# Slack for named consumers in an engine plan, a second buffer for the second products, and places of sorted tokens counted in two levels

## The chip, the core and the metric

The kernel runs on one core of one Trainium2 chip. The engines of the core run side by side, each with an instruction queue of its own that is worked off in order: TensorE (PE in the profile; PEld is its weight loading), VectorE (DVE), ScalarE (ACT), GpSimd (POOL) and SyncE (SP), which here only issues DMAs. The metric is the device time of one execution in microseconds. The time before is 2369.66 us, the median of three runs (2361.89 to 2370.21).

## The reference, cut to what matters

```python
# x: 32 images, 128 channels, 56 x 56 pixels, float32
x = x + conv3x3(sign(group_norm(x)), sign(w)) * Alpha        # w from M, Z, rv
t = x as tokens                                              # 32 x 3136 x 128
n = layer_norm(t)
t = t + (n @ Wq + bq) * sum_over_tokens((n @ Wk + bk) * (n @ Wv + bv))
n = layer_norm(t)
p = softmax(n @ router_w + router_b)                         # 8 experts
top_p, top_i = top_k(p, 2);  top_p = top_p / sum(top_p)
t = t + sum_k top_p[k] * (n @ expert_w[top_i[k]] + expert_b[top_i[k]])
x = t as images
```

## The kernel before, in words

**Units.** An image has 3136 tokens, cut into 25 chunks of 128 (the last has 64) and 7 blocks of four chunks (the last has one). The images form four groups of 8, 8, 8 and 4 (`GROUPS`), and four more that belong to no group.

**The first part of an image.** Its two halves are loaded (L296), the sum and the sign of the group norm are taken on ScalarE (`gn_sum` L511, `gn_sign` L531), the convolution is 7 x 9 matmuls (L565), which VectorE adds to x (L576). PE turns x into tokens (`to_tokens` L592), ScalarE copies them out (L598), VectorE takes statistics (L605). ScalarE scales the tokens (L656), PE sums their products (`gram` L665), some small steps (`kv_1` to `kv_8`) make the vector that the queries are multiplied with, and `project` (L780) with its two followers (L794, L806) ends the attention.

**The experts, two ways.** The router is computed on VectorE. The first 8 chunks of an image in groups 0 and 1, the first 12 in groups 2 and 3 (`DENSE`) and all 25 of the last four images take the dense way: for each block and each pair of experts, SP issues a DMA that spreads two rows of gates over the partitions (`spread`, tile `bc`, L1044), VectorE multiplies the turned tokens with them (`gated`, L1053, two buffers), and PE multiplies by the two expert matrices (`experts`, L1071, into the bank `ff`).

The other chunks (17 or 13 per image) take the sorted way. `pair_of` on VectorE numbers the pair of experts of each token (28 pairs) and writes a 0/1 array `hot` (chunk x pair, L1163). `places` on PE counts, by matmuls into one bank, how many tokens of the same pair come ahead of a token: one matmul with a triangle for the chunk's own tokens (L1174), two for the images before (L1177), and for each chunk c one with ones that adds its counts to all later chunks (L1186). ScalarE copies the new counts (`count_on`), VectorE forms row numbers (`row_numbers`), and GpSimd scatters the tokens to their rows in DRAM (L1253).

When a group is sorted, its rows are read back as tiles of 128 rows of one pair, four tiles (a quad) at a time, 40, 40, 32 and 20 quads in the groups. The steps of a quad are:

- `tile_load`, SP: four DMAs (L1517) into `t_in`, three buffers
- `tile_turn`, PE: four transposes (L1524); `tile_turned`, ScalarE: the copy out (L1530, tile `turned`, two buffers)
- `tile_experts`, PE, in two halves: products with the two expert matrices of the pair (L1542, tile `to`)
- `tile_read`, ScalarE, in two halves: the first products scaled and shifted into `v` (L1560), the second scaled into `w` (L1567, one buffer)
- `tile_sum` and `tile_out`, VectorE: v + w (L1572) and the tokens added (L1577)
- `tile_store`, SP: the store to `res` (L1585)

Then GpSimd gathers the results of each image (`gather`, L1323, rows found by `result_rows`), PE turns them (`back_turn`, L1338), ScalarE copies them out (`back_out`, L1346, tile `o`) and SP stores them (L1350).

**The order.** The order of every engine's queue is made on the host, ahead of the build. Each step is announced with `at(...)`: a due time, its engine, a guess of its work, the steps that it comes `after`, the rings of buffers that it takes (`take`) and frees (`free`), and a `delay` after which a DMA counts as landed. `in_order` plays this plan through: on each engine it takes, of the steps that could start about now, the one with the earliest due time. A step can start when what it waits for is done, plus a hop of 0.5 to 0.8. `ROOM` says how many buffers of each ring the plan counts on. The plan decides nothing but the order: on the chip each instruction starts when its engine has come to it and its semaphores are there. The line that the change edits in `in_order` is

```python
f.ready = max(f.ready, clock[s.engine] if same else s.done + HOP[f.engine])
```

where s is the step just placed and f one that waits for it; `same` is true when both are on one engine.

## Time and profile before

The profiled execution took 2367.37 us, with a span of 2365.7 us from its first to its last instruction; 1.7 us lie around the span.

| engine | busy us | share of the span | instructions |
|---|---|---|---|
| PE | 2146.5 | 91% | 12074 |
| DVE | 1959.7 | 83% | 6332 |
| ACT | 1519.5 | 64% | 4883 |
| POOL | 1029.2 | 44% | 971 |

The mean granted TensorE clock is 0.971 of full speed. Matmuls are pipelined and their ends are modelled, so a busy PE need not be PE at its peak. The groups that the change is about:

| group | count | busy us | mean ns |
|---|---|---|---|
| PE L1186, matmuls of `places` | 428 | 51.8 | 276 |
| PE L1542, products of the quads | 2112 | 291.8 | 286 |
| ACT L1530, turned quads copied | 132 | 81.1 | 616 |
| ACT L1560, first products | 528 | 252.9 | 479 |
| ACT L1567, second products | 528 | 206.0 | 390 |
| DVE L1572, v + w | 132 | 90.8 | 688 |
| DVE L1053, gated, 128 x 1024 | 368 | 445.6 | 1214 |
| DVE L1163, `hot`, 128 x 476 | 16 | 10.3 | 646 |

A float32 matmul is recorded as two instructions, so 2112 records are 1056 products. An engine that waits does so in its own order: whatever is queued behind the waiting instruction waits with it.

### The profile page before, as it was taken

What the parts mean: (1) busy time and instruction counts of PE and PEld (TensorE: products, weight loads), DVE (VectorE), ACT (ScalarE), POOL (GpSimd) and SP (SyncE); (2) the same over time, 40 slices, a digit from 0 to 9 for tenths busy, and PEclk for the clock granted to TensorE, in tenths of its full rate; (3) what the DMA queues carried; (4) which work ended last, traced back from release to release, by engine and by line L of the source; (5) the groups of instructions that cost most, each with busy time, mean ns of one, the idle gap of its engine ahead of it and who ended that gap; (6) DMA issues with size and microseconds to landing.
All of it is one profiled execution on the core that took longest, in us unless ns stands there. A gap on an engine that the chain in (4) does not pass through costs nothing.

```text
span 2365.7 us, 44856 instructions
## 1 busy us (share of the span) xinstructions
PE 2146.5 (91%) x12074; PEld 1476.3 (62%) x12074; DVE 1959.7 (83%) x6332; ACT 1519.5 (64%) x4883; POOL 1029.2 (44%) x971
## 2 busy tenths in 40 slices
PE   4999999998999989998999999999998989989878
PEld 2766656566677666666676676666667656665533
DVE  4899999998988877997788878999877787778755
ACT  5767765567877777667777766666777846563311
POOL 1054443432333313755544454666644553343562
PEclk9999999999999999999999999999999999999989
DMA  4155434465564544576667766677676766867678
GB/s 163 43 176 176 151 131 136 153 192 152 178 187 151 156 134 143 170 228 205 202 206 218 214 174 195 221 221 255 202 236 172 240 193 203 261 207 231 212 225 272
DMA packets 317739, 448.55 MB, mean 190 GB/s; under 512 B 61065, under 2 KB 223153, under 8 KB 317490
## 3 DMA queue, kind: packets, MB, share of 16 engines
q1 hardware_dynamic: 289090, 386.97, 52.3%
q0 software_dynamic: 27392, 55.17, 7.8%
q10 hardware_dynamic: 1008, 3.54, 0.4%
q8 instruction: 101, 1.65, 0.3%
q14 instruction: 148, 1.21, 0.2%
HBM read 319.51 MB, written 126.00 MB: 188 GB/s over the span
## 4 chain that ended last, share of the span: by engine, by line
PE 35%; DVE 19%; DMA 11%; ACT 9%; issue 5%; SPq 2%; POOL 1%; DVEq 0%; ACTq 0%; POOLq 0%
PE ff L1071 12%; PE cv L565 6%; PE to L1542 4%; DVE gated L1053 4%; PE gram L665 3%; PE q L780 3%; DMA back<-res,res_no 3%; DMA x<-in_x_dram 2%; DMA bc<-gp 2%; ACT v L1560 2%; DVE tok L732 2%; ACT w L1567 2%; ACT y L656 1%; DVE st L605 1%; DMA rows<-tok,row_no 1%
## 5 line engine op out<-in xcount | busy, mean ns | idle before, releaser
L1253 POOL DMA_INDIRECT rows<-tok,row_no x428 | 523.7, 1223 | 780.3 <-issue 221.8
L1071 PE MATMUL ff<-gated,ew_d 128*128 128x512 f32 (+1 forms) x1536 | 719.8, 597 | 34.2 <-DVE gated L1053 34.1
L1323 POOL DMA_INDIRECT back<-res,res_no x428 | 496.2, 1159 | 519.7 <-PE back_ps L1338 335.0
L1053 DVE TENSOR_TENSOR gated<-tt,bc 128x1024 f32<-128x1024 f32 x384 | 450.1, 1175 | 66.7 <-PE ff L1071 52.3
L565 PE MATMUL cv<-xs,w_bin 128*128 128x448 bf16 x2016 | 433.6, 359 | 10.0 <-ACT w L1567 4.6
L1071 PEld LDWEIGHTS ff<-gated,ew_d 128*128 128x128 f32 x1536 | 274.7, 194 | 263.0 <-issue 189.6
L1542 PE MATMUL to<-ew_s,turned 128*128 x2112 | 291.8, 286 | 50.4 <-ACT turned L1530 46.3
L1542 PEld LDWEIGHTS to<-ew_s,turned 128*128 128x128 f32 x2112 | 269.8, 198 | 91.7 <-ACT turned L1530 59.6
L1560 ACT ACTIVATE v<-to,t_in 128x128 f32<-128x128 f32 x528 | 252.9, 479 | 109.0 <-PE to L1542 106.2
L794 ACT ACTIVATE qs<-q,r 128x136 f32<-128x136 f32 (+1 forms) x800 | 247.7, 406 | 98.7 <-PE q L780 91.0
L565 PEld LDWEIGHTS <-w_bin 128*128 128x128 bf16 x2016 | 197.4, 99 | 175.5 <-issue 28.1
L656 ACT ACTIVATE y<-tok,r 128x128 f32<-128x128 f32 (+1 forms) x800 | 250.9, 411 | 52.9 <-DVE r L476 42.0
L665 PEld LDWEIGHTS gram<-y 128*128 128x128 f32 (+1 forms) x1600 | 212.0, 197 | 61.3 <-ACT y L656 31.1
L780 PE MATMUL q<-move,x 128*128 128x144 f32 (+1 forms) x1600 | 237.2, 292 | 8.4 <-ACT w L1567 7.1
L665 PE MATMUL gram<-y 128*128 128x129 f32 (+1 forms) x1600 | 226.5, 286 | 14.7 <-ACT y L656 14.7
L780 PEld LDWEIGHTS q<-move,x 128*128 128x128 f32 (+1 forms) x1600 | 212.6, 191 | 34.7 <-issue 14.6
L1567 ACT ACTIVATE w<-to,t_in 128x128 f32<-128x128 f32 x528 | 206.0, 390 | 3.7 <-DVE v L1572 3.7
L605 DVE BATCH_NORM_STATS2 st<-tok 128x6 f32<-128x128 f32 (+1 forms) x800 | 180.5, 276 | 23.6 <-ACT tok L598 22.8
L1572 DVE TENSOR_TENSOR v<-v,w 128x512 f32<-128x512 f32 x132 | 90.8, 688 | 122.0 <-ACT w L1567 121.5
L813 DVE BATCH_NORM_STATS2 st<-tok 128x6 f32<-128x128 f32 (+1 forms) x800 | 189.1, 276 | 0.0
L598 ACT COPY tok<-xt 128x512 f32<-128x512 f32 (+1 forms) x224 | 118.1, 566 | 75.2 <-PE xt L592 71.6
L576 DVE SCALAR_TENSOR_TENSOR x<-cv,alpha_col,x 128x448 f32<-128x448 f32 x224 | 150.9, 674 | 16.6 <-PE cv L565 14.7
(214 smaller groups left out, 2935.0 us busy)
## 6 DMA issues: line engine op xcount, KB each, us to landing
bc<-gp SPq DMA_DIRECT2D x368, 512.0 KB
x<-in_x_dram SPq DMA_DIRECT2D x64, 784.0 KB
t_in<-rows SPq DMA_DIRECT2D x528, 66.0 KB
res<-v SPq DMA_DIRECT2D x132, 256.0 KB
out_dram<-o SPq DMA_DIRECT2D x100, 256.0 KB
out_dram<-tt SPq DMA_DIRECT2D x92, 256.0 KB
rows<-zeros SPq DMA_DIRECT2D x116, 66.0 KB
rows<-tok,row_no POOLq DMA_INDIRECT x428
```

The lines of the kernel that those rows point to most:

```text
L565: nc.tensor.matmul(cv, lhsT=w_bin[:, t, :], rhs=xs[:, b * ROWS + dy : b * ROWS + dy + ROWS, dx : dx + width], start=(t == 0), stop=(t == T ...
L656: nc.scalar.mul(y[:n, j, :C], d["tok"][:n, c, :C], d["r1"][:n, c : c + 1])
L665: nc.tensor.matmul(d["gram"], lhsT=y[:n, j, :C], rhs=y[:n, j, :], start=(c == 0), stop=(c == n_ck - 1),)
L780: nc.tensor.matmul(p[:n, k, :], lhsT=d["x"][:, c * C : c * C + n], rhs=move, start=True, stop=True,)
L794: nc.scalar.mul(qs[:n, k, : C + N_EXP], p[:n, k, : C + N_EXP], d["r1"][:n, c : c + 1])
L1053: nc.vector.tensor_tensor(g[:, :, :n], d["tt", b][:, :n].unsqueeze(1).to_broadcast([C, 2, n]), d.pop(("bc", b, k))[:, :, :n], ALU.mult,)
L1071: nc.tensor.matmul(d["ff", b][:, :n], lhsT=ew_d[:, e * C : (e + 1) * C], rhs=g[:, j, :n], start=False, stop=(e == N_EXP - 1),)
L1253: dma = nc.gpsimd.indirect_dma_start(out=groups[group]["rows"], out_offset=bass.IndirectOffsetOnAxis(ap=d["row_no"][:n, c - n_dense : c - ...
L1323: dma = nc.gpsimd.indirect_dma_start(out=d["back", c][:n, :], out_offset=None, in_=groups[group]["res"][: quads_of(group) * WIDE, :], in_o ...
L1542: nc.tensor.matmul(p[:, k, j, :], lhsT=t[:, n * C : (n + 1) * C], rhs=ew_s[:, bass.ds(d["cols", q][j][n], C)], start=True, stop=True,)
L1560: nc.scalar.activation(d["v", q][:, n, :], p[:, k, 0, :], AF.Identity, bias=row[:, C + 2 : C + 3], scale=row[:, C : C + 1],)
L1567: nc.scalar.mul(d["w", q][:, n, :], p[:, k, 1, :], row[:, C + 1 : C + 2])
```

## The change

A step gets one more number, `slack`. In the plan a step on another engine can start only `slack` later than it could before; the chip does not see it, only the order moves. It is 2.0 for `tile_read`, 1.0 for `tile_turned` and 0.5 for `gated`. The time at which a ring's buffer comes free in the plan is not moved by it. `tile_turn` of a quad is now placed after the second half of `tile_experts` two quads back. The `delay` of the loads of x goes from 9 to 13.

The tile `w` gets two buffers, in the plan and on the chip. The tile `o` goes from three buffers on the chip to the two that the plan counted on.

`pair_of` gets one more VectorE instruction, a reduction of `hot` over each four chunks (`hot_sum`, bfloat16). `places` adds the counts of a chunk only to the later chunks of its own four, and the sum of four to all chunks behind them. The guesses of work for both now go with the number of chunks.

```diff
@@ -84,16 +84,17 @@
 BANKS, EMPTIES = ("ps", "acc", "ff"), 7.0
 ROOM = dict(
     x=3, tok=3, ps=5, acc=1, ff=2, y=3, qs=3, tt=4, bc=4, gt=2, gated=2,
-    t_in=3, turned=2, v=3, w=1, back=12, sent=4, o=2,
+    t_in=3, turned=2, v=3, w=2, back=12, sent=4, o=2,
 )
 
 
 class Step:
 
 
-    def __init__(self, due, key, engine, work, do, args, after, take, free, delay):
+
+    def __init__(self, due, key, engine, work, do, args, after, take, free, delay, slack):
         self.due, self.key, self.engine, self.work = due, key, engine, work
-        self.do, self.args, self.delay = do, args, delay
+        self.do, self.args, self.delay, self.slack = do, args, delay, slack
         self.after, self.take, self.free = after, take, free
         self.done = None
 
@@ -156,7 +157,7 @@
             missing[f.key] -= 1
 
             same = f.engine == s.engine and (not s.delay or f.key[0] == s.key[0])
-            f.ready = max(f.ready, clock[s.engine] if same else s.done + HOP[f.engine])
+            f.ready = max(f.ready, clock[s.engine] if same else s.done + s.slack + HOP[f.engine])
             if not missing[f.key]:
                 waiting.setdefault(f.engine, []).append(f)
     return order
@@ -403,6 +404,7 @@
 
 
     hot_all = const.tile([C, most + 1, N_PAIR], BF16, name="hot")
+    hot_sum = const.tile([C, most // PER, N_PAIR], BF16, name="hot_sum")
 
     def prepare_sorted():
         nc.gpsimd.memset(hot_all, 0.0)
@@ -437,8 +439,8 @@
 
     steps = {}
 
-    def at(due, key, engine, work, do, *args, after=(), take=(), free=(), delay=0.0):
-        steps[key] = Step(due, key, engine, work, do, args, after, take, free, delay)
+    def at(due, key, engine, work, do, *args, after=(), take=(), free=(), delay=0.0, slack=0.0):
+        steps[key] = Step(due, key, engine, work, do, args, after, take, free, delay, slack)
 
     def base(i):
 
@@ -538,7 +540,7 @@
         at(
             s - 60, ("load", i), "SP", 0.1, load,
             after=[("load", i - 1)] + ([("gn_sign", 0, GN_PARTS - 1)] if i == 1 else []),
-            take=["x"], delay=9.0 if i else 19.0,
+            take=["x"], delay=13.0 if i else 19.0,
         )
         for j in range(GN_PARTS):
             rows = j * height // GN_PARTS, (j + 1) * height // GN_PARTS
@@ -1116,7 +1118,7 @@
                     begin + n * unit, ("gated", i, n), "DVE", 1.14 * share, gated, b, k,
                     after=[("spread", i, n), ("tt_out", i, b)]
                     + [("gated", i, n - 1) if n else ("gated", i - 1, last_unit)],
-                    take=["gated"], free=[("bc", ("spread", i, n))],
+                    take=["gated"], free=[("bc", ("spread", i, n))], slack=0.5,
                 )
                 at(
                     begin + n * unit + 2, ("experts", i, n), "PE",
@@ -1143,6 +1145,7 @@
         first_of_group = i == 0 or group_of[i - 1] != group
         sort = slice(n_dense, n_ck)
         hot = hot_all[:, most - n_sort :, :]
+        n_full = n_sort // PER
 
         def pair_of():
             high, low, pair = (
@@ -1166,6 +1169,13 @@
                 pair_no.unsqueeze(1).to_broadcast(shape),
                 ALU.is_equal,
             )
+            with nc.allow_low_precision(reason="numbers up to four"):
+                nc.vector.tensor_reduce(
+                    hot_sum[:, :n_full, :],
+                    hot[:, : n_full * PER, :].rearrange("p (b k) q -> p b q k", k=PER),
+                    AX.X,
+                    ALU.add,
+                )
 
         def places():
 
@@ -1181,14 +1191,17 @@
                         start=False,
                         stop=False,
                     )
-            for c in range(n_sort):
-                n = n_sort - c
+
+            counted = [(hot[:, c, :], c + 1, min(n_sort + 1, c // PER * PER + PER)) for c in range(n_sort)]
+            counted += [(hot_sum[:, b, :], (b + 1) * PER, n_sort + 1) for b in range(n_full)]
+            counted = [(t, lo, hi) for t, lo, hi in counted if lo < hi]
+            for t, lo, hi in counted:
                 nc.tensor.matmul(
-                    p[:, c + 1 :, :],
+                    p[:, lo:hi, :],
                     lhsT=ones_h,
-                    rhs=hot[:, c, :].unsqueeze(1).to_broadcast([C, n, N_PAIR]),
+                    rhs=t.unsqueeze(1).to_broadcast([C, hi - lo, N_PAIR]),
                     start=False,
-                    stop=c == n_sort - 1,
+                    stop=lo == counted[-1][1] and hi == counted[-1][2],
                 )
             d["places"] = p
 
@@ -1261,11 +1274,11 @@
             alone(f"rows{group}", dma, in_turn(dma))
 
         at(
-            s + 132, ("pair_of", i), "DVE", 0.87, pair_of,
+            s + 132, ("pair_of", i), "DVE", 0.9 + 0.03 * n_sort, pair_of,
             after=[("route_3", i), ("row_numbers", i - 1), ("places", i - 1), ("result_rows", i - 13)],
         )
         at(
-            s + 133, ("places", i), "PE", 2.1, places,
+            s + 133, ("places", i), "PE", 0.3 + 0.08 * n_sort, places,
             after=[("pair_of", i), ("count_rest", i - 1), ("list_1", group - 1)], take=["ps"],
         )
         at(s + 135, ("count_rest", i), "DVE", 0.11, count_rest, after=[("count_on", i)])
@@ -1342,7 +1355,7 @@
 
         def back_out(b):
             lo, hi = cols_of(b)
-            d["o", b] = bpool.tile([C, WIDE], F32, tag="o", name=f"o_{i}_{b}")
+            d["o", b] = bpool.tile([C, WIDE], F32, tag="o", bufs=2, name=f"o_{i}_{b}")
             nc.scalar.copy(d["o", b][:, : hi - lo], d.pop(("back_ps", b))[:, : hi - lo])
 
         def back_store(b):
@@ -1552,7 +1565,7 @@
         d = groups[g]
         if h == 0:
             d["v", q] = bpool.tile([C, PER, C], F32, tag="v", name=f"v_{g}_{q}")
-            d["w", q] = bpool.tile([C, PER, C], F32, tag="w", bufs=1, name=f"w_{g}_{q}")
+            d["w", q] = bpool.tile([C, PER, C], F32, tag="w", bufs=2, name=f"w_{g}_{q}")
         p = d.pop(("to", q, h))
         for k in range(2):
             n = 2 * h + k
@@ -1624,11 +1637,12 @@
             )
             at(
                 due, ("tile_turn", g, q), "PE", 0.45, tile_turn, g, q,
-                after=[("tile_load", g, q), ("tile_turn", g, q - 1)], take=["ps"],
+                after=[("tile_load", g, q), ("tile_turn", g, q - 1), ("tile_experts", g, q - 2, 1)],
+                take=["ps"],
             )
             at(
                 due + 1, ("tile_turned", g, q), "ACT", 0.47, tile_turned, g, q,
-                after=[("tile_turn", g, q)], take=["turned"], free=[("ps", ("tile_turn", g, q))],
+                after=[("tile_turn", g, q)], take=["turned"], free=[("ps", ("tile_turn", g, q))], slack=1.0,
             )
             for h in range(2):
                 at(
@@ -1639,7 +1653,7 @@
                 at(
                     due + 3 + 2 * h, ("tile_read", g, q, h), "ACT", 1.40, tile_read, g, q, h,
                     after=[("tile_experts", g, q, h), ("tile_read", g, q, h - 1)],
-                    take=[] if h else ["v", "w"], free=[("ps", ("tile_experts", g, q, h))],
+                    take=[] if h else ["v", "w"], free=[("ps", ("tile_experts", g, q, h))], slack=2.0,
                 )
             at(
                 due + 9, ("tile_sum", g, q), "DVE", 0.60, tile_sum, g, q,
```

## The prediction

> **What bounds the kernel now.** I read the page's busy times and slices first, then the waits by engine, then the stretches in which tiles are read back, then the chain.
>
> ```profile
> PE 2146.5 (91%) x12074; PEld 1476.3 (62%) x12074; DVE 1959.7 (83%) x6332; ACT 1519.5 (64%) x4883; POOL 1029.2 (44%) x971
> PE   4999999998999989998999999999998989989878
> PEclk9999999999999999999999999999999999999989
> PE 35%; DVE 19%; DMA 11%; ACT 9%; issue 5%; SPq 2%; POOL 1%; DVEq 0%; ACTq 0%; POOLq 0%
> ```
>
> PE is busy nearly everywhere, and the chain of work has PE as its largest owner, but with many short stays on other engines: PE is the bound, with stalls. It was idle for 2365.7 - 2146.5 = 219 us; 29 of them lie at the start. The waits say whom it waited for (engine, line, releaser: us in total, times, longest):
>
> ```profile
> PE to L1542 <- ACT turned L1530: 46.3, 23, 5.5
> PE ff L1071 <- DVE gated L1053: 34.1, 27, 4.1
> PE places L1174 <- DVE hot L1163: 14.0, 11, 2.8
> PE q L780 <- ACT w L1567: 7.1, 4, 2.8
> PE cv L565 <- ACT w L1567: 4.6, 4, 2.5
> DVE v L1572 <- ACT w L1567: 121.5, 59, 5.9
> ACT w L1567 <- DVE v L1572: 3.7, 4, 2.1
> ACT o L1346 <- DMA out_dram<-o: 44.6, 10, 11.4
> ACT junk L511 <- DMA x<-in_x_dram: 39.9, 19, 6.0
> SPq L1517 <- DVE v L1577: 202.3, 66, 10.0
> ```
>
> The largest stall of PE is a quad's product waiting for its turned tile. VectorE stands 121.5 us in front of the sum of a quad. SP stands 202.3 us in front of quad loads, until `t_in` is free. By stretches (length; busy of PE, PEld, DVE, ACT, POOL; clock, DMA share, GB/s):
>
> ```profile
> 540.00:900.00 360.00, 328.06 (x2024) 245.61 (x2023) 300.78 (x971) 274.08 (x886) 109.18 (x88) 0.95 0.54 163
> 1080.00:1440.00 360.00, 331.53 (x2040) 244.99 (x2041) 289.38 (x889) 265.47 (x840) 168.34 (x148) 0.98 0.68 202
> 60.00:540.00 480.00, 449.39 (x2530) 300.68 (x2529) 450.62 (x1688) 325.02 (x1096) 189.65 (x149) 0.98 0.46 147
> 1440.00:1680.00 240.00, 233.75 (x1269) 153.34 (x1268) 232.21 (x800) 151.53 (x498) 147.76 (x120) 0.99 0.68 222
> ```
>
> The first two are stretches with tile reading: PE loses 9 and 8%, and no other engine is over 84%. The last two have none: PE and VectorE are both at 94 to 97%, and nothing much can be won there.
>
> **Turned tiles: 27 us won (10 to 42).** What hides the copy of a turned quad is the PE work queued between `tile_turn` and the first `tile_experts`. From the order of both kernels and the trace's durations (convolution 1.83, gated pair 1.74, `gram` block 0.89, half a quad 0.90, `project` 0.74, transposes 0.44) this cover has a mean of 3.2 us before and 3.9 after; it is below 2.0 in 27 of 132 quads before and in none after, below 2.5 in 45 and 6. The copy takes 0.62 itself, so what made 23 quads wait 2.0 each is copies queued behind other ACT work. If waits go with the quads below 2.5, 23 x 6/45 = 3 stay, 6 us: 40 won, and with the 1.9 us that the same line shows under issue at most 42. If ACT's queue is what is late, a median cover grown by 0.9 (2.9 to 3.8) takes 23 x 0.9 = 21 off; 10 is half of that. I take 27.
>
> **Places: 10 us won (-16 to +25), and 3 at its start (0 to 9).** With 17 chunks, L1186 adds 17 x 18/2 = 153 chunk columns of 28; after, 25 in thirteen narrow matmuls and 32 in four wide ones. With 13 chunks it is 91 against 37. The instructions stay at 17 and 13. Seventeen took 2.0 us in the trace for 4284 columns. Whether narrow ones are cheap:
>
> ```profile
> L1186 PE MATMUL places<-hot,ones_h x10: 175/229/282, 872.4 to 873.1; 128*128 128x280 bf16 x1, 128*128 128x252 bf16 x1, 128*128 128x224 bf16 x1, 128*128 128x196 bf16 x1
> ```
>
> The last ten, 280 columns down to 28, start within 0.7 us, and nine of them stream 1512 columns, 0.46 ns each: no floor shows down to some 30 ns. So an image with 17 comes to 1596 x 0.46 = 0.73, and 0.1 for the floor: 1.1 us less, or 0.6 less with 13. 16 x 1.1 + 12 x 0.6 = 25 us of PE, the upper bound. [...]
>
> VectorE pays for the reduction. The trace has no such form; the nearest row is the reduction of 476 float32 elements to 17 (L1207), 647 ns, hence 0.61 for 448 elements and 0.46 for 336: 16 x 0.61 + 12 x 0.46 = 15 us, 16 as the loss if VectorE is the bound throughout and PE's gain is worth nothing. It is not: only 11 of 28 images (0 to 6 and some four later) fall in stretches where VectorE is as full as PE. There I count the two as even. The other 17 keep 25 x 17/28 = 15, less about a third for places where another wait ends last: 10. PE need not wait for the reduction: the triangle, the two counts and thirteen narrow matmuls, over 1 us, read `hot` alone. The plan's guess for `pair_of` rises from 0.87 to 1.41, so `places` is put later behind it, against the 14.0 us (11 times) that PE waits for `hot`; 3 of these.
>
> **Slack of 2.0 behind readings, and two `w`: 8 us won (0 to 30).** Between the end of a reading and its sum the plan now puts 3.6 VectorE steps on average (2.0 before), so most of the 121.5 us goes. It is idle time of an engine that is not the bound there (84%). PE pays for it only where it waits for VectorE in these stretches: `gated` 7.4 in the second, and about as much in `kv_ps` and the like: 5 (0 to 15). The second `w` removes 3.7 us of ScalarE waits and lets readings start earlier, and these hold the banks that PE waits for (4.6 + 7.1 + 2.9 on other lines = 14.6): 3 (0 to 15).
>
> **Slack of 0.5 behind `gated`: 3 us won (-5 to +12).** The 27 waits have a mean of 1.3, so half a microsecond takes at most 27 x 0.5 = 13 off; the last 100 us alternate between these two engines whatever the order. A later product frees its `gated` buffer later in the plan, hence the loss.
>
> **Clock: 4 us won (0 to 15).** The granted clock is 0.95 and 0.98 in the reading stretches above and 0.99 in a full one. 4 and 1% of 360, and about 2% of the third of 240, are 23 us of clock; a stall costs clock only around it, so 4. [...]
>
> **Load delay: 1 us won (0 to 4).** ScalarE's 39.9 us before `junk` are time of an engine at 64%; without that cover they would cost what PE waits for `xs`, 4.1.
>
> **Two `o` for three: 3 us lost (0 to 13).** ScalarE already stands 44.6 us, all of it after 2260, since stores sit on SP behind gate spreads (L1044). Behind the waiting copy are copies of `tt`, which VectorE's `gated` and so PE need. ScalarE is busy for only 6.65 of the 60 us from 2280 to 2340, and `tt` waits for stores of its own (29.9 us). One buffer less lets each of the 10 waits begin one copy earlier, about 5 us; a quarter of 10 x 5 is 13; I take 3.
>
> **Later end of the readings: 5 us lost (0 to 15).** The last product of group 2 moves back by 15 steps of PE, of group 3 by 17. Group 3's first gather has over 100 us of PE work in between. For group 2 the cover up to its first `back_turn` falls from about 62 to 47 us, at a place where late gathers already held VectorE (7.6 us at once) and through it PE (6.8 us). GpSimd's queue keeps its order; SP's quad loads move back by 2 on average, which puts spreads ahead of them.
>
> **Sum.** -27 - 10 - 3 - 8 - 3 - 4 - 1 + 3 + 5 = -48 on the profiled 2367.4, to 2319. The median of the runs is 2.3 above that execution: 2322.
>
> **The rivals.**
> A, the stalls move: PE's 46.3 us come back in front of other instructions, since ScalarE and VectorE are each at 76 to 84% in these stretches and every step moved there moves another. Then places (13) are left: 2357. For it: PE waits in over thirty ways in this trace; against it: 46.3 in one of them.
> B, all of it arrives: 42 + 25 + 9 + 12 + the banks' 15 - 16 for the reduction = 87 off: 2283.
> C, the slower one: SP's wait for `t_in`. Its three buffers are freed by `tile_out`, which moves back with the 2.0 of slack. If each of the 66 waits grows by 2.0, SP stands 132 us longer, and the spreads queued behind each quad load come late; VectorE waits for spreads 11.7 us now. It overtakes the gains (48) when 36% of the 132 reaches PE. At 55% it is 73 - 48 = 25 slower: 2395. Against it: the plan moves quad loads behind spreads, not before.
>
> **How the numbers follow.** Likeliest 0.53, own range 2295 to 2350; A 0.20, B 0.15, C 0.12. The bounds above, taken as independent, add to about 32 either way, 2290 to 2354; stretched to B's edge and over A into the near part of C, 2286 to 2374 leaves no more than 2 in 10 out. A change under 0.5% (12 us) can't be told from none. Half of A is faster by more and half is not: faster 0.78, same 0.10, slower 0.12.
>
> **What would show it.** After the change, PE's wait for the turned tile should be under 20 us, VectorE's for `w` under 50, L1186 some 25 us shorter between its first and last starts, a reduction of 0.5 to 0.6 us x28 on VectorE, and the clock in the reading stretches up by 0.01. C would show as VectorE's wait for spreads above 50; A as a sum of PE's idle time that stays near 219. The prediction is wrong if PE's idle time falls and the span doesn't, for then PE was not what ends the stretches.

## The result, and the profile after

The changed kernel takes 2340.69 us (median of 4 runs, 2338.41 to 2347.18) against 2369.84 for the kernel before on the same chip (4 runs, 2361.89 to 2370.21): a ratio of 0.9889 [0.986, 0.9919], 29 us less. In a second session it took 2343.22 against 2372.34 (0.9872 [0.9851, 0.9894]). In two of the three sessions of the experiments below every kernel, the one before too, was some 8% slower (2565 and 2557 for the kernel before), with stalls that the profile puts down to no instruction of the program (119 us of VectorE's idle time in e3's trace, up to 16.8 at once, for 9 in the changed kernel's first trace), so kernels are compared only within a session; the second session was like the first measurement.

The page of the changed kernel: its span, the busy times, PE's slices, the granted clock and the chain.

```profile
span 2340.6 us, 45031 instructions
PE 2129.5 (91%) x12074; PEld 1466.5 (63%) x12074; DVE 1973.8 (84%) x6360; ACT 1518.5 (65%) x4883; POOL 1053.7 (45%) x971
PE   4999999899999999999999999999889889979888
PEclk9999999999999999999999999999999899989989
PE 35%; DVE 20%; DMA 11%; ACT 10%; issue 3%; SPq 1%; POOL 1%; DVEq 0%; ACTq 0%; POOLq 0%
```

PE is still the bound. The span fell by 25.1 us, of which 17.0 are busy time of PE (2146.5 to 2129.5) and only 8 its idle time (219 to 211). The dips in PE's slices at the tenth, fifteenth and nineteenth, which lay in the readings of groups 0 and 1, are gone, and a new one stands at the eighth; of the last twelve slices eight are below 9 where six were, and the clock dips there in three.

The waits of the changed kernel (engine, line, releaser: us in total, times, longest); 1055, 1073, 1184, 1555, 1580 and 1585 are the lines 1053, 1071, 1174, 1542, 1567 and 1572 of before:

```profile
PE ff L1073 <- DVE gated L1055: 54.3, 27, 9.3
PE to L1555 <- ACT turned L1543: 26.6, 13, 4.2
PE places L1184 <- DVE hot L1166: 15.7, 12, 2.9
PE q L782 <- ACT w L1580: 6.5, 5, 2.3
PE cv L567 <- ACT w L1580: 2.0, 2, 1.7
DVE v L1585 <- ACT w L1580: 98.4, 54, 7.0
ACT o L1359 <- DMA out_dram<-o: 45.6, 13, 7.7
ACT junk L513 <- DMA x<-in_x_dram: 34.7, 17, 5.0
SPq L1530 <- DVE v L1590: 191.3, 68, 9.0
DVE res_no L1331 <- DMA back<-res,res_no: 38.2, 7, 12.8
DVE gated L1055 <- DMA bc<-gp: 18.8, 9, 7.3
SPq L1530 <- DMA rows<-tok,row_no: 13.4, 2, 12.2
PE turn L1537 <- ACT w L1580: 6.6, 1, 6.6
```

Three lines of the kernel before that belong beside them:

```profile
DVE res_no L1318 <- DMA back<-res,res_no: 21.0, 7, 7.6
DVE gated L1053 <- DMA bc<-gp: 11.7, 6, 3.6
SPq L1517 <- DMA rows<-tok,row_no: 6.3, 2, 5.3
```

The wait for the turned tile fell from 46.3 us to 26.6, the wait for `gated` rose from 34.1 to 54.3. Their sum is 80.4 before and 80.9 after; in the second session's traces it is 80.8 for the kernel before (with two buffers more of `res_no`, which change nothing for it, e7 below) and 79.7 for the changed one. The equal sums hide changes in different places, the fall above all from 510 to 1410 and the rise outside it:

| PE's wait, us, before → after | 0–510 | 510–1410 | 1410–1640 | 1640–2110 | 2110–end |
|---|---|---|---|---|---|
| for `turned` | 0 → 0 | 31.0 → 18.5 | 1.8 → 0 | 13.5 → 8.2 | 0 → 0 |
| for `gated` | 4.2 → 7.6 | 9.9 → 8.3 | 0.5 → 4.6 | 3.2 → 13.9 | 16.3 → 19.9 |

The stretches of the changed kernel (length; busy of PE, PEld, DVE, ACT, POOL; clock, DMA share, GB/s), the first four as shown of before, then two more, the last from `places` of image 24 to those of image 25:

```profile
540.00:900.00 360.00, 337.81 (x2127) 251.51 (x2126) 318.60 (x1037) 287.85 (x940) 113.44 (x93) 0.98 0.56 169
1080.00:1440.00 360.00, 342.37 (x2125) 250.62 (x2125) 307.37 (x939) 270.18 (x863) 188.36 (x155) 0.99 0.67 205
60.00:540.00 480.00, 448.73 (x2529) 300.55 (x2530) 453.12 (x1695) 324.20 (x1094) 187.95 (x146) 0.95 0.45 146
1440.00:1680.00 240.00, 225.83 (x1229) 148.07 (x1230) 220.76 (x743) 149.89 (x482) 155.23 (x125) 0.97 0.69 220
60.00:510.00 450.00, 420.61 (x2347) 280.23 (x2348) 424.02 (x1604) 304.26 (x1026) 172.71 (x136) 0.95 0.45 146
1583.10:1661.10 78.00, 66.64 (x365) 46.00 (x364) 64.33 (x209) 45.74 (x145) 50.53 (x42) 0.91 0.63 199
```

The last two of the kernel before, the second again from image 24 to image 25, which lie later in it:

```profile
60.00:510.00 450.00, 420.86 (x2357) 280.68 (x2355) 422.55 (x1607) 304.69 (x1028) 172.24 (x136) 0.98 0.46 147
1621.90:1693.60 71.70, 67.25 (x386) 46.42 (x385) 62.90 (x206) 48.00 (x154) 45.31 (x37) 0.98 0.70 223
```

In the two reading stretches PE is 10 and 11 us busier and the clock 0.03 and 0.01 higher. From 60 to 510 PE's busy time is what it was, at a clock lower by 0.03. Between `places` of image 24 and of image 25 the changed kernel takes 6.3 us longer for much the same work, at a clock lower by 0.07. From 510 on the same clock times hold other work in the two kernels. So the same events in four traces, two of each kernel, have to say where the time went (us from the span's start):

| event | before | before, six `res_no` (e7) | after | after (e5) | mean shift |
|---|---|---|---|---|---|
| `places` of image 8 | 513.3 | 517.5 | 515.7 | 518.1 | +1.5 |
| last quad store of group 0 | 921.3 | 926.0 | 902.1 | 901.0 | −22 |
| last quad store of group 1 | 1447.7 | 1448.9 | 1407.8 | 1401.6 | −44 |
| `places` of image 24 | 1621.9 | 1623.0 | 1583.1 | 1577.6 | −42 |
| first quad store of group 2 | 1677.8 | 1680.7 | 1650.8 | 1645.7 | −31 |
| 59th load of `x` | 1764.4 | 1765.5 | 1728.8 | 1723.4 | −39 |
| last quad store of group 2 | 1917.8 | 1918.2 | 1909.9 | 1904.2 | −11 |
| 65th dense store | 1947.0 | 1947.8 | 1921.0 | 1914.8 | −29 |
| end | 2365.7 | 2366.1 | 2340.6 | 2337.0 | −27 |

Nothing is won in the first 510 us, where two traces of one kernel differ by 4. The readings of groups 0 and 1 bring some 42, and 15 of these are lost again behind image 24. The change also moves the quads' steps against the other work, so a single event of the later part does not tell the place. PE's idle time between the same events does (length less PE's busy time; PE's instructions agree within 6% in the stretch to `places` of image 25 and within 2% in the others):

| PE's idle time, us | before | e7 | after | e5 |
|---|---|---|---|---|
| 60 to `places` of image 8 | 30.5 | 32.1 | 31.2 | 30.3 |
| to the last quad store of group 1 | 73.4 | 71.0 | 49.9 | 47.6 |
| to `places` of image 24 | 3.3 | 3.5 | 4.2 | 3.9 |
| to `places` of image 25 | 4.4 | 6.2 | 11.4 | 12.2 |
| to the 65th dense store | 26.5 | 25.8 | 31.3 | 30.3 |
| to the end | 50.1 | 47.9 | 52.0 | 52.5 |

In the readings of groups 0 and 1 PE waits 23 us less. Some 14 us more come behind image 24, where PE has run ahead of DMAs that did not come as much earlier. The timeline of the changed kernel:

```profile
1614.47 1.23 DVE L1055 TENSOR_TENSOR gated<-tt,bc 128x1024 f32<-128x1024 f32 x1 [7.31 <-DMA bc<-gp]
1615.75 3.78 PE L1073 MATMUL ff<-gated,ew_d 128*128 128x512 f32 x4 [4.60 <-DVE gated L1055]
1913.06 0.98 POOL L1336 DMA_INDIRECT back<-res,res_no  x1 [10.64 <-PE cv L567]
2054.47 0.17 DVE L1331 TENSOR_TENSOR res_no<-by,place 128x13 uint32<-128x13 f32 x1 [8.01 <-DMA back<-res,res_no]
2061.35 3.62 PE L1073 MATMUL ff<-gated,ew_d 128*128 128x512 f32 x4 [9.30 <-DVE gated L1055]
2218.76 0.17 DVE L1331 TENSOR_TENSOR res_no<-by,place 128x13 uint32<-128x13 f32 x1 [6.71 <-DMA back<-res,res_no]
2220.80 3.78 PE L1073 MATMUL ff<-gated,ew_d 128*128 128x512 f32 x4 [6.20 <-DVE gated L1055]
```

At 1608 SP stands 12.2 us in front of the first quad load of group 2, since the last scatters of that group's rows have not landed (5.3 at most before, 8.1 in e7). The gate spread queued behind it comes late, VectorE waits 7.31 us for it, and PE 4.60. At 2054 and 2219 VectorE waits for the gathers of four images back before it may write new row numbers, `gated` is queued behind, and PE waits 9.30 and 6.20. These three waits add up to 20.1 us, as much as the rise of the wait for `gated`. GpSimd's first gather of group 2, at 1913, had waited 10.64 us, and it starts 3.2 us after that group's last quad store was issued (the profile names a convolution here; in e8's trace the same wait of 10.58 us is put down to the store). Besides, PE stands 6.6 us once in front of a quad's transposes, near 1644.

What the counting costs now, VectorE's reductions by shape (busy us, mean ns of one):

```profile
L1173 DVE TENSOR_REDUCE hot_sum<-hot 128x112 bf16<-128x448 bf16 x16 | 14.4, 900 | 0.0
L1173 DVE TENSOR_REDUCE hot_sum<-hot 128x84 bf16<-128x336 bf16 x12 | 8.5, 711 | 0.0
```

Together 22.9 us. PE's count matmuls fell from 51.8 us of busy time to 25.5, by 26.3, which is the whole fall of PE's busy time and some 9 more.

### The profile page after: what moved, and what is told of

Its sections match the earlier page's. It is cut to its first block, busy times and chain, and to the rows that moved or that the text cites. A ratio compares the mean times of both kernels' runs of the same rounds, so it can differ in the third digit from the quotient of the medians.

```text
span 2340.6 us, 45031 instructions
## 1 busy us (share of the span) xinstructions
PE 2129.5 (91%) x12074; PEld 1466.5 (63%) x12074; DVE 1973.8 (84%) x6360; ACT 1518.5 (65%) x4883; POOL 1053.7 (45%) x971
## 4 chain that ended last, share of the span: by engine, by line
PE 35%; DVE 20%; DMA 11%; ACT 10%; issue 3%; SPq 1%; POOL 1%; DVEq 0%; ACTq 0%; POOLq 0%
PE ff L1073 11%; PE cv L567 6%; PE to L1555 5%; DVE gated L1055 5%; PE q L782 3%; DMA back<-res,res_no 2%; DMA bc<-gp 2%; PE gram L667 2%; ACT y L658 2%; ACT v L1573 2%; DMA t_in<-rows 2%; PE xt L594 2%; ACT w L1580 2%; DVE st L607 1%; DVE x L578 1%
## 5 line engine op out<-in xcount | busy, mean ns | idle before, releaser
L1266 POOL DMA_INDIRECT rows<-tok,row_no x428 | 537.7, 1256 | 771.8 <-issue 336.8
L1073 PE MATMUL ff<-gated,ew_d 128*128 128x512 f32 (+1 forms) x1536 | 722.5, 598 | 54.9 <-DVE gated L1055 54.3
L1336 POOL DMA_INDIRECT back<-res,res_no x428 | 506.6, 1184 | 485.0 <-PE back_ps L1351 284.4
L567 PE MATMUL cv<-xs,w_bin 128*128 128x448 bf16 x2016 | 438.6, 363 | 8.2 <-ACT xs L533 4.6
L1555 PE MATMUL to<-ew_s,turned 128*128 x2112 | 286.9, 286 | 28.9 <-ACT turned L1543 26.6
L1585 DVE TENSOR_TENSOR v<-v,w 128x512 f32<-128x512 f32 x132 | 90.6, 687 | 105.0 <-ACT w L1580 98.4
L578 DVE SCALAR_TENSOR_TENSOR x<-cv,alpha_col,x 128x448 f32<-128x448 f32 x224 | 150.8, 673 | 17.8 <-PE cv L567 16.3
```

The source lines that it names most:

```text
L567: nc.tensor.matmul(cv, lhsT=w_bin[:, t, :], rhs=xs[:, b * ROWS + dy : b * ROWS + dy + ROWS, dx : dx + width], start=(t == 0), stop=(t == T ...
L1073: nc.tensor.matmul(d["ff", b][:, :n], lhsT=ew_d[:, e * C : (e + 1) * C], rhs=g[:, j, :n], start=False, stop=(e == N_EXP - 1),)
L1266: dma = nc.gpsimd.indirect_dma_start(out=groups[group]["rows"], out_offset=bass.IndirectOffsetOnAxis(ap=d["row_no"][:n, c - n_dense : c - ...
L1336: dma = nc.gpsimd.indirect_dma_start(out=d["back", c][:n, :], out_offset=None, in_=groups[group]["res"][: quads_of(group) * WIDE, :], in_o ...
L1555: nc.tensor.matmul(p[:, k, j, :], lhsT=t[:, n * C : (n + 1) * C], rhs=ew_s[:, bass.ds(d["cols", q][j][n], C)], start=True, stop=True,)
```

## The experiments

First session (the kernel before: 2565.36, 7 runs, 2542.11 to 2573.3).

**e1_places_only**: the kernel before, with the two-level places alone (reduction, matmuls and the plan's two guesses).

```diff
+            with nc.allow_low_precision(reason="numbers up to four"):
+                nc.vector.tensor_reduce(
...
-            for c in range(n_sort):
-                n = n_sort - c
+            for t, lo, hi in counted:
...
-            s + 132, ("pair_of", i), "DVE", 0.87, pair_of,
+            s + 132, ("pair_of", i), "DVE", 0.9 + 0.03 * n_sort, pair_of,
```

> The kernel before with the two-level count of places alone (its guesses of work in the plan too). Theory: the narrow matmuls save PE some 25 us in all, but the reduction costs VectorE 28 x 0.82 = 23 us (measured in the changed kernel, 697 to 919 ns), and in the stretches without tile reading VectorE is as full as PE; so little is left: 0 to 8 us faster than before, ratio 0.997 to 1.000, with the seven images up to 510 us not faster at all. Rival, places carry the result: 15 us or more faster, ratio 0.994 or less.

2571.01 (2532.04 to 2577.12), 1.002 by the medians. One run took 2532 and three 2570 or more, so there is no interval and nothing follows; it was repeated (e9).

**e2_plan_only**: the changed kernel with the count of before: slack, turned tiles, gating, loads and buffers alone.

```diff
-            counted = [(hot[:, c, :], c + 1, min(n_sort + 1, c // PER * PER + PER)) for c in range(n_sort)]
...
+            for c in range(n_sort):
+                n = n_sort - c
```

> The changed kernel with the count of places as it was before (one level, no reduction, old guesses of work): the four slacks, the load delay, the two buffers of w and the two of o remain. Theory, the plan carries the result: 20 to 28 us faster than before, ratio 0.988 to 0.992. Rival, places carry half of it or more: 5 to 15 us faster, ratio 0.994 to 0.998.

2517.69 (2512.76 to 2537.36), 0.9846 [0.9768, 0.9924]. Here the plan's part is worth some 1.5%, and PE's wait for the turned tile is still 35.8 us, 18 times, and the one for `gated` 35.6.

**e3_turned_only**: the kernel before, with the later `tile_turn`, the slack of 1.0 behind it, two `w` and two `o`; no other slack, the load delay and the count of before.

```diff
+                after=[("tile_load", g, q), ("tile_turn", g, q - 1), ("tile_experts", g, q - 2, 1)],
...
+                after=[("tile_turn", g, q)], take=["turned"], free=[("ps", ("tile_turn", g, q))], slack=1.0,
```

> Of the plan's part only the slack of 1.0 behind turned tiles, the new place of the transposes and the two buffers of w (and two of o); no slack behind readings and gating, the old load delay, the old count of places. Theory, PE's wait for turned tiles is what was won: PE's wait for the turned tile falls from 46 to 30 us or less, and the time is 12 to 22 us below before, ratio 0.991 to 0.995. Rival, the slack of 2.0 behind readings is what helps (VectorE's wait for w fell from 121 to 98 us): under 6 us faster, ratio above 0.997.

2511.9 (2509.11 to 2515.58), 0.981 [0.9747, 0.9874]: as good as the whole plan part or better, and more than the 12 to 22 us expected. Its waits:

```profile
PE ff L1072 <- DVE gated L1054: 47.2, 33, 6.7
PE to L1545 <- ACT turned L1533: 21.1, 13, 3.7
```

Thirteen waits for the turned tile stay, as in the changed kernel, and the wait for `gated` is at 47.2 with only the turned tiles moved (and two `w` and two `o`), where e9, with the old plan, has 31.1. They may have a part in it: no wait for `gated` in e3, e10 or e11, which have no slack behind readings, is over 7.0, while the 9.30 of the changed kernel comes back in e5, e6 and e8 (7.4 to 8.8). But e2, which has that slack and the turned tiles, has 5.3 at most and 35.6 in all. Which part raises it is open.

**e4_res_no_6**: the changed kernel with six buffers of `res_no` for four, since VectorE's wait for late gathers had grown from 21.0 to 38.2 us.

```diff
-            d["res_no"] = spool.tile([C, n_sort], U32, tag="res_no", bufs=4, name=f"res_no_{i}")
+            d["res_no"] = spool.tile([C, n_sort], U32, tag="res_no", bufs=6, name=f"res_no_{i}")
```

> The changed kernel with six buffers for the gathers' row numbers instead of four, so that VectorE need not wait for the gathers of four images back when it writes the next numbers; the order is unchanged. Theory, this wait (38 us on VectorE, 12.8 at once near 1900, PE behind it 7.4 at once) gives back part of the gain from 1850 on: VectorE's wait for the gathers falls below 10 us, PE's wait of 7 us near 1900 is gone, and the time is 6 to 14 us below the changed kernel: 2326 to 2335, ratio to before 0.982 to 0.986. Rival, the gathers themselves are late and the wait only moves to the transposes behind them: within 4 us of the changed kernel, ratio 0.987 to 0.991.

2480.13 (2452.98 to 2509.49), 0.972 [0.9633, 0.9807]. It is the fastest of the first session, but the changed kernel itself had not run there, so it was repeated beside it (e6).

Second session (the kernel before: 2372.34, 13 runs, 2363.46 to 2377.34).

**e5_after_again**: the changed kernel as it is, for the comparisons of the second session.

> The changed kernel as it is, beside the others of this call, so that they can be set against it on one chip; on the chip of the first four runs the kernel before took 2565 us, with single stalls of up to 16 us that no releaser in the profile explains, and the changed kernel did not run there. Expected on a chip without these: ratio to before 0.986 to 0.992.

2343.22 (2338.71 to 2345.28), 0.9872 [0.9851, 0.9894].

**e6_res_no_6b**: e4's edit, here.

> The changed kernel with six buffers for the gathers' row numbers instead of four, again, now beside the changed kernel. Theory, VectorE's wait for the gathers gives back part of the gain from 1850 on: 6 to 14 us below the changed kernel of this call. Rival, the gathers themselves are late and the wait only moves: within 4 us of it.

2333.11 (2329.27 to 2336.97), 0.9832 [0.981, 0.9855], 10 us below e5. The stalls that it should remove are these, first of e5 (VectorE's timeline: start, length, then in brackets the idle time before it):

```profile
1893.55 0.17 DVE L1331 TENSOR_TENSOR res_no<-by,place 128x13 uint32<-128x13 f32 x1 [12.48 <-DMA back<-res,res_no]
2213.76 0.17 DVE L1331 TENSOR_TENSOR res_no<-by,place 128x13 uint32<-128x13 f32 x1 [7.40 <-DMA back<-res,res_no]
```

and of e6:

```profile
1894.00 0.17 DVE L1331 TENSOR_TENSOR res_no<-by,place 128x13 uint32<-128x13 f32 x1 [14.39 <-DMA back<-res,res_no]
2151.43 0.17 DVE L1331 TENSOR_TENSOR res_no<-by,place 128x13 uint32<-128x13 f32 x1 [5.39 <-DMA back<-res,res_no]
```

The stall near 1894 stays, with two buffers more: it moved from image 19 to image 21, which now waits for image 15's gathers as image 19 did. Image 15 is the last of group 1, whose products were all stored by 1402, so this stall does not come from the later end of group 2. In the first traces VectorE comes to this place 34 us earlier than before (1887.4 for 1921.0), while image 15's last gather ends only 28 earlier (1898.6 for 1927.0); why GpSimd gains less is open. The stall at 2213 is gone, with the 6.9 us that PE waited behind it, and there e6 wins: it is 1.8 us ahead of e5 at the 83rd dense store (2203.8 in e5) and 10.6 at the 85th (2236.6). So more buffers help the tail; at 2047 VectorE still stands 7.3 us in front of row numbers, and PE 8.7 behind it.

**e7_before_res_no_6**: the same edit to the kernel before.

> The kernel before with six buffers for the gathers' row numbers. VectorE waited 21 us there before (28 to 38 us after the change, with 12.8 at once in place of 7.6). Theory, the wait got worse through the change, as group 2's readings end later: here the gain is smaller than in the changed kernel, 0 to 7 us. Rival, the wait was as costly before the change and has nothing to do with it: the same gain as in the changed kernel.

2370.18 (10 runs, 2365.16 to 2375.84), 0.9996 [0.9981, 1.0012]. Four buffers cost the kernel before nothing; what six bring after the change is a cost that came with it.

**e8_pair_adds**: the changed kernel, with two additions of neighbours in place of the reduction over four.

```diff
-                nc.vector.tensor_reduce(
...
+            two = hot_sum[:, : 2 * n_full, :]
+            pairs = hot[:, : n_full * PER, :].rearrange("p (b k) q -> p b k q", k=2)
+            nc.vector.tensor_add(two, pairs[:, :, 0, :], pairs[:, :, 1, :])
+            halves = two.rearrange("p (b k) q -> p b k q", k=2)
+            nc.vector.tensor_add(hot_four[:, :n_full, :], halves[:, :, 0, :], halves[:, :, 1, :])
```

> The changed kernel with the sums of four chunks made by two additions of neighbours (bfloat16, 224 or 168 and then 112 or 84 results) in place of the strided reduction, which took 697 to 919 ns. Theory, the narrow matmuls of places save PE 25 us and the reduction's 23 us of VectorE eat it in the stretches where VectorE is full: the two additions take 0.2 to 0.3 us each, 9 us of VectorE less in all, and the time is 2 to 8 us below the changed kernel, with the first 510 us 3 us shorter or more. Rival, VectorE's cost is hidden: within 2 us of it.

2330.73 (2316.01 to 2334.75), 0.9823 [0.9797, 0.9848], 12.5 us below e5 by the medians, more than the 2 to 8 expected; the ratios differ by 0.5% with some 0.35% either way. Its additions:

```profile
L1175 DVE TENSOR_TENSOR hot_sum<-hot 128x224 bf16<-128x224 bf16 x16 | 4.2, 265 | 0.0
L1177 DVE TENSOR_TENSOR hot_four<-hot_sum 128x112 bf16<-128x112 bf16 x16 | 3.2, 201 | 0.0
L1175 DVE TENSOR_TENSOR hot_sum<-hot 128x168 bf16<-128x168 bf16 x12 | 2.8, 232 | 0.0
L1177 DVE TENSOR_TENSOR hot_four<-hot_sum 128x84 bf16<-128x84 bf16 x12 | 2.4, 198 | 0.0
```

They take 12.6 us where the reductions took 22.9: 10.3 less on VectorE, and about as much comes off the time. Its trace (its fastest run, 2316.0, where the other three took 2327 to 2335) wins in the first 510 us, where VectorE is full: `places` of image 8 starts at 508.3, 7 to 10 us before the changed kernel's two. It is still 8.7 us ahead of e5 at `places` of image 24 and 18.3 at that of image 25. This second step is the late spread of the changed kernel: SP stands at most 3.5 us for scatters here, and the 7.9 us of VectorE and 5.2 of PE that e5 loses near 1610 are not there. That the additions brought this about is not shown. From 60 to 510:

```profile
60.00:510.00 450.00, 420.02 (x2383) 280.64 (x2382) 427.95 (x1639) 310.19 (x1049) 176.34 (x136) 0.97 0.45 147
```

All engines but GpSimd get through more instructions than in the changed kernel (PE 2383 against 2347, VectorE 1639 against 1604), at a clock of 0.97 against 0.95.

Third session (the kernel before: 2557.22, 7 runs, 2547.07 to 2574.08).

**e9_places_only_b**: e1 again.

> The kernel before with the two-level count of places alone, again, on a chip without the unexplained stalls of the first four runs. Theory, VectorE's reduction (23 us in all) uses up what the narrow matmuls save PE (25 us): 0 to 5 us faster than before, ratio 0.998 to 1.000, and 3 us slower in the first 510 us. Rival, places carry a third or more of the result: 10 us or more faster, ratio 0.996 or less.

2538.24 (2529.14 to 2552.34), 0.9899 [0.9841, 0.9957]. With e1 beside it, the places alone bring between nothing and 1%: inconclusive.

**e10_turned_only_b**: e3 again.

> Of the plan's part only the slack of 1.0 behind turned tiles, the new place of the transposes and the two buffers of w (and two of o), again, beside the changed kernel's parts. Theory, this is all that won: 20 to 32 us faster than before, ratio 0.987 to 0.992, as fast as the whole change or faster. Rival, the slacks behind readings and gating add their share: 10 to 18 us faster, ratio 0.9925 to 0.996.

2508.7 (2497.26 to 2514.31), 0.9781 [0.9724, 0.9837], with waits of 22.7 us for the turned tile and 47.2 for `gated`. This repeats e3.

**e11_read_slack_0**: the changed kernel without the slack behind readings.

```diff
-                    take=[] if h else ["v", "w"], free=[("ps", ("tile_experts", g, q, h))], slack=2.0,
+                    take=[] if h else ["v", "w"], free=[("ps", ("tile_experts", g, q, h))], slack=0.0,
```

> The changed kernel without the slack of 2.0 behind readings. Theory, this slack buys VectorE idle time that nobody needed and makes the readings of group 2 end later: without it the time is 0 to 8 us below the changed kernel's 2343, ratio to before 0.984 to 0.988, and VectorE's wait for w goes back above 105 us. Rival, it is worth its prediction of 5 us or more: 5 us or more above, ratio 0.989 or higher.

2499.11 (2484.26 to 2513.16), 0.9739 [0.9672, 0.9806]. The changed kernel did not run in the third session, so there is no direct price of the slack; but without it the kernel is no slower than e10, and VectorE's wait for `w` is 83.1 us, not above 105 as expected and less than the 98.4 that the changed kernel shows in its first trace. GpSimd's first gather of group 2 has nothing to wait for here (0.3 us), and the wait for `gated` is 39.0 us.

**e12_best**: the changed kernel with e8's additions and e6's buffers.

> The changed kernel with both improvements found: the sums of four chunks by two additions of neighbours in place of the reduction, and six buffers for the gathers' row numbers. Theory, the two act in different stretches (everywhere up to 1900, and after 2200) and add up: 18 to 24 us below the changed kernel's 2343, ratio to before 0.977 to 0.981. Rival, what one takes away the other has already: 10 to 14 us below, ratio 0.982 to 0.984.

2471.3 (2457.59 to 2490.09), 0.9632 [0.9562, 0.9701]: the fastest here, 1.5% below e10. It beats the kernel before by 3.7%; the changed kernel, which e8 and e6 beat alone in the second session, did not run in this one.

## Why the prediction was right, and where its terms were wrong

The direction, and the likeliest case's own range (2295 to 2350), held: 2340.7, 29 us won for 48 forecast. Its main step is seen in the traces: with the turned tiles and the counts PE waits and works less in the readings of groups 0 and 1, and at `places` of image 24 the changed kernel was 42 us ahead, near the 48. Behind that 15 were lost again, for which the sum has 5. That the end still lies inside the range is a balance of terms off in both directions, and partly luck.

**Turned tiles, 27 in the sum.** The step that failed is "if waits go with the quads below 2.5, 23 x 6/45 = 3 stay". Thirteen stay, in the changed kernel and in e3, and the wait shrank by 19.7 us: close to the 21 of the other reading, that ScalarE's queue is late. The cover was counted in PE's steps, but the copy waits for its turn on ScalarE, which had no idle time ahead of any of the 13 copies that PE waited for. The larger error is that the whole term was carried to the end. In the readings of groups 0 and 1 PE's idle time fell by 23 us, of which the wait for the turned tile made 14 (32.8 to 18.5 us there) and the wait of `gram` for `y` some 7 (8.5 to 1.6), which no term of the sum names; behind image 24 some 14 came back, and with them the wait for `gated` rose by 20.2. The sign that was named for rival A is there: PE's idle time fell only from 219 to 211. Its mechanism is not: what came back are waits for a late spread and late gathers, not steps of ScalarE and VectorE in the stretches where the turned tiles were moved. A's time of 2357 is 16 off and the forecast 19, so the truth lies between the two. e3 and e10 show that the turned tiles, with two `w` and two `o`, pay 2% in the first and the third session.

**Gating slack, 3 of 13.** It brought nothing that the traces show: the waits are 27 as before, with a mean of 2.0 us for 1.3. It was not tried alone.

**Places, 10 and 3.** PE's side was sized well: 25 as the upper bound, 26.3 measured. An image with 17 chunks takes 0.95 us from the first start to the last end where it took 2.02, with 1.1 less forecast; its thirteen narrow matmuls start within 0.40 us where their 700 columns at 0.46 ns make 0.32, so the 0.1 allowed for a floor was about right. VectorE's side was off by half, 22.9 for 15: the price was borrowed from a reduction over contiguous float32, and this one is over bf16, in groups of four, and steps through its operand; no run separates these. "There I count the two as even" held for the first 510 us (+1.5, within the spread of 4), where the count matmuls of nine images save PE 12.4 us, and e8 shows that a cheaper reduction wins there. The 3 for the wait for `hot` fell out: 14.0 became 15.7, whatever the guess in the plan. Outside those nine images 13.9 of PE's 26.3 us are left, and with 8 of idle time they make 22 of the 25 us that the profiled span lost. This is an account of the two traces and no direct trial of the two parts; e1 and e9 leave the places alone open.

**Readings, 5 and 3.** VectorE's wait for `w` went from 121.5 to 98.4, not below 50; the slack of the plan did not become slack on the chip. ScalarE's 3.7 us behind the single `w` are gone, as forecast. The waits for banks fell little (4.6 to 2.0, 7.1 to 6.5), and a new one of 6.6 stands in front of the transposes.

**Clock, 4.** Up by 0.03 and 0.01 in the reading stretches, as said, but down by 0.03 from 60 to 510, and between `places` of image 24 and of image 25 from 0.98 to 0.91; over the run 0.971 became 0.966 (0.969 and 0.966 in the second session). So the term has the wrong sign. "A stall costs clock only around it" fits the traces: from 60 to 510 each spell of half the clock lasts 3.4 us and begins within 2.1 us after a wait of PE of 1.4 to 2.9 us (last section). That 4 of the 23 us would come was the author's estimate.

**Later end of the readings, 5 of 15.** The term was tied to the stall near 1900, and that was a misreading: image 19's row numbers wait there for the gathers of image 15, which belongs to group 1, stored by 1447.7 before and 1407.8 after. The timeline of the changed kernel, VectorE's first instruction after it and PE's:

```profile
1900.12 0.17 DVE L1331 TENSOR_TENSOR res_no<-by,place 128x13 uint32<-128x13 f32 x1 [12.77 <-DMA back<-res,res_no]
...
1906.41 1.12 PE L594 MATMUL xt<-ident,x 128*128 128x128 f32 x4 [7.37 <-DVE x L578]
```

VectorE stands for 12.77 us in front of the row numbers, and `x` for PE's next transposes is queued behind it. Before, the longest such wait was 7.6, but PE then stood 6.8 us behind it (6.5 in e7) and now 7.4 (4.5 in e5), so little is lost here. The later end shows further on. Group 2's last quad store is only 11 us earlier than before; the first gather of the group, which before had 0.3 us of idle time ahead of it, waits 10.6 for it (9.3 to 10.6 in e5, e6 and e8); and VectorE's wait for the gathers of image 19, at 2054, costs PE 9.3 us (7.4 in e5) where VectorE waited 0.5 before. So the cover of 47 us did not suffice. What this costs in time is not shown: PE's idle time from the 65th dense store to the end grew by some 3 us, and an earlier end of group 2's readings was not tried by itself (e11 moves it, in a session where it can't be priced).

**Two `o`, −3; loads, 1.** ScalarE's waits for stores of `o` are 45.6 for 44.6 us: no loss. Its waits for `x` fell from 39.9 to 34.7, and nothing shows it in the time. Three `o` in the changed kernel were not tried.

**The rivals.** B fell with what came back behind image 24. C did not happen at its price: SP's wait for `t_in` is 191.3 for 202.3, and VectorE's wait for spreads is 18.8, well under the 50 named. But its path, a spread held up behind a quad load, shows once: near 1608, with 4.6 us of PE, by a wait for scatters and not for `t_in`.

Open: the weights of the two parts in a session like the second, the reading and the gating slack by themselves, and why GpSimd's scatters and gathers do not come as much earlier as PE's work.

## What to carry to other kernels

Where PE and VectorE were both full (94% from 60 to 510), work moved from one to the other won nothing that shows (+1.5 us at `places` of image 8), so price the new form by a run of that form (2.0 ns an element here, where the form it was priced by took 1.4) and try cheaper ones: here two additions (12.6 us) beat one reduction (22.9) and brought about as much as they saved. A wait removed by a better order is won only if the sum of the engine's idle time falls (here from 219 to 211); compare that time between the same events of both traces, since the same clock times hold other work, and two sums of waits can be equal by chance (80.4 and 80.9 here). PE, running ahead, met the DMAs that did not come as much earlier (three waits, 20.1 us): look for what stands in a queue in front of the next load, spread or gather. Slack that moves a stream back can move its end too (the first gather of group 2 waits 10.6 us for it, and 0.3 in e11, without the slack behind readings): look at who gathers from it first.

## What the runs showed of the hardware

A reduction over groups of four with a step of 28 bf16 between the four took 900 ns for 448 elements, 2.0 ns each, where the contiguous float32 one of 476 took 647, 1.4 ns each. Additions of 224 and 112 bf16 results took 265 and 201.

The narrow matmuls of `places` follow each other closely. The timeline of the changed kernel, PE (start, length):

```profile
157.54 0.55 PE L1199 MATMUL places<-hot,ones_h 128*128 128x84 bf16 x13
157.94 0.55 PE L1199 MATMUL places<-hot_sum,ones_h 128*128 128x392 bf16 x4
```

Thirteen of 28 to 84 columns start within 0.40 us, 31 ns each.

The granted clock falls to 0.50 in spells of 3.4 us or a multiple of it: of the 37 within the span of the changed kernel's trace, 28 last 3.4 us, eight 6.8 and one 10.2. Two stretches of the changed kernel (columns as above):

```profile
226.00:228.30 2.30, 0.78 (x3) 0.43 (x3) 2.30 (x6) 1.55 (x6) 2.00 (x2) 1.00 0.85 164
228.30:231.70 3.40, 3.40 (x6) 1.34 (x5) 2.89 (x9) 3.40 (x10) 2.79 (x3) 0.50 1.00 412
```

PE had stood 1.52 us for `gated` until 227.6. From 60 to 510 the trace's record of the clock has 12 such spells (13 in e5) where the kernel before has 5 (6 in e7): this is the 0.95 against 0.98. Each of the 12 and of the 5 begins within 2.1 us after a wait of PE of 1.4 to 2.9 us; some other waits as long are followed by none (1.50 us until 431.6 and 1.63 until 460.0 in the changed kernel). In the wait of 7.4 us near 1900 the clock falls at 1904.2, before the wait ends at 1906.4, and is 0.50 until 1911.0.
